# Keys of seven blocks by a seven-product scheme, with sums of x made by adding transfers

## The chip, the cores and the metric

The kernel runs on one core of one Trainium2 chip. The metric is device time in microseconds; a kernel's time is the median of its runs. Engines are named as in the profile: PE (matmul), PEld (its weight loads), DVE (vector), ACT (scalar), POOL and SP (here only issuers of transfers).

## What is computed

Two non-local blocks follow one another on x of 4 x 128 x 96 x 96, float32. Each does the following for every image:

```python
g_x     = maxpool2(conv1x1(x, g_w, g_b))          # 64 x 2304, after pooling
theta_x = conv1x1(x, theta_w, theta_b)            # 64 x 9216
phi_x   = maxpool2(conv1x1(x, phi_w, phi_b))      # 64 x 2304
f    = einsum('bqc,bck->bqk', theta_x, phi_x)     # 9216 queries, 2304 keys
attn = softmax(f, axis=-1)
y    = einsum('bqk,bkc->bqc', attn, g_x)
out  = conv1x1(y, W_w, W_b) * inv + (bn_beta - bn_mean * inv) + x
```

Four images and two layers make eight blocks. What the text calls the keys of a block is phi_x and g_x together: a 128 x 128 weight (64 rows of g, 64 of phi) times 9216 pixels, and a 2 x 2 maximum.

## The kernel before

**Blocks, pairs, steps.** The eight blocks stand in the order (image, layer) 00, 10, 01, 20, 11, 30, 21, 31. A block has 9 pairs; a pair is two tiles of 512 queries. The program is one loop over t, 648 steps; a pair takes 9 steps (NB), each with two tiles (KB) of 128 keys. Two pairs make a cycle of 18 steps (CYCLE); s is t modulo 18. Instruction order on PE, DVE, ACT and SP is that of the program; each engine takes its own in that order and waits by semaphores.

**A step.** `scores` of two key tiles (PE, L400), each followed by `exp` (ACT, L406); between the two stands `first`, a slot for other PE work, and after them `second`. Then `add_up` of the two exp tiles (DVE, L415), with a slot `take` between them that evacuates what PE made in the slots. Then `values` (PE, L423) of the two key tiles of the step before. Behind these come the tail pieces: `turn` (transposes and reduces of the exp sums, s = 8, 9 and 4, 5), `add_halves` (12 and 2), `invert` (13 and 6), `normalise` (1 and 10), each for the even and the odd pair, and transposes of keys.

**Quarters of the array.** Every matmul is 64 rows by 64 columns, so four run side by side. `scores` and `values` issue one for each quarter. A float32 matmul of the program is two records in the profile.

**The slots.** `thetas` of two pairs at s = 5 and 6; the W matmuls (`multiply`, L517) at s = 3 and 12, with ACT adding the shift (L528) and POOL adding the result to x in place by an adding transfer (L532); and keys.

**Keys before.** The keys of block n + 1 are made while block n runs. A chunk is 512 pixels, 128 keys; `chunks` does two of them with four matmuls in `first` and four in the next step's `second` (L236), into the two banks of the pool `ps_misc` that theta and W use as well. `take` reduces each bank by the 2 x 2 maximum into a tile `gphi` (DVE, L262). There are nine such calls a block, three in a cycle (`KEYS = (15, 17, 31)`), so keys take three of every four or five cycles. Every third call is followed by `centred` and `copied` (ACT, L336 and L342: phi less its mean, into both halves of the partitions of `phi`) and by `square` (DVE, L353: 32 x 32 transposes of g into `gT`). Block 0's keys are made at the start.

**Denominators.** `invert` sends the reciprocals by SP as two rows into the tile `turned` (L496) and from there, each row to 64 partitions, into half of `halves` (L501). `normalise` waits for that.

**Pools.** exp tiles have `EXPS = 7` buffers, `halves` two, `ps_sc` two double banks.

Of the kernel before, what the change touches and what calls it, by code (L numbers as in the profile page):

```python
# [16 lines left out]
P = 128  # L17
# [7 lines left out]
GT = 6  # L25
# [9 lines left out]
KB = 2  # L35
NB = NKT // KB
FIRST = 6
KEYS = (15, 17, 31)
THETAS = 5


TURNS, HALVES, INVERT = (8, 4), (12, 2), (13, 6)
NORM, PROJECT = (1, 10), (3, 12)
SQ = 32
EXPS = 7
WARM = (5, 3)
CYCLE = 2 * NB
ORDER = ((0, 0), (1, 0), (0, 1), (2, 0), (1, 1), (3, 0), (2, 1), (3, 1))
# [5 lines left out]
def shifted_blocks(ctx: ExitStack, tc: tile.TileContext, x: bass.AP, layers, out: bass.AP, flag):  # L54
# [47 lines left out]

    notes = const.tile([P, len(ORDER) * NP + 1, 2], F32, name="notes")
    nc.vector.memset(notes, 0.0)
    limits = const.tile([P, 2], F32, name="limits")
    for i, limit in enumerate((SUM_MAX, 1.0 / SUM_MIN)):
        nc.vector.memset(limits[:, i : i + 1], limit)
# [29 lines left out]
    class Layer:  # L137
# [3 lines left out]
            self.l, self.p, self.col = l, p, {}  # L141

        def load_gphi(self, engines):
            self.gphi_nat = prep.tile([2 * CI, C], F32, name=f"gphi_nat_{self.l}")
            for i, key in enumerate(("g", "phi")):
                engines[i].dma_start(out=self.gphi_nat[ts(i, CI), :], in_=self.p[f"{key}_w"])

        def load_theta(self, engine):
            self.theta_nat = prep.tile([CI, C], F32, name=f"theta_nat_{self.l}")
            engine.dma_start(out=self.theta_nat, in_=self.p["theta_w"])  # L150

        def load_W(self, engine):
            self.W_nat = prep.tile([C, CI], F32, name=f"W_nat_{self.l}")
            engine.dma_start(out=self.W_nat, in_=self.p["W_w"])
            self.g_b = prep.tile([C, CI], F32, name=f"g_b_{self.l}")
            engine.dma_start(out=self.g_b, in_=self.p["g_b"].partition_broadcast(C))

        def make_std(self):
# [15 lines left out]
        def steps_gphi(self):  # L174
            self.gphi = const.tile([C, 2 * CI], F32, name=f"gphiT_{self.l}")
            return turned(self.gphi, self.gphi_nat)

        def steps_theta(self):
            self.theta = const.tile([C, CI], F32, name=f"thetaT_{self.l}")
            return turned(self.theta, self.theta_nat)  # L180

        def steps_W(self):

            self.W = const.tile([2 * CI, C], F32, name=f"WT_{self.l}")
            self.W_bn = prep.tile([C, CI], F32, name=f"W_bn_{self.l}")
            self.inv = prep.tile([C, 1], F32, name=f"inv_{self.l}")
            twice = lambda: nc.scalar.copy(self.W[CI:, :], self.W[:CI, :])
            return [self.make_scale] + turned(self.W[:CI, :], self.W_bn) + [twice, self.make_shift]
# [51 lines left out]
    class Block:  # L240


        def __init__(self, xt, w, store, name):
            self.xt, self.w, self.store, self.name = xt, w, store, name

        def begin_keys(self):
            name = self.name
            self.gphi = kvp.tile([P, NK], F32, tag="gphi", name=f"gphi_{name}", bufs=1)
            self.phi = kvp.tile([P, NK], F32, tag="phi", name=f"phi_{name}")
            self.gT = kvp.tile([P, NKT, CI], F32, tag="gT", name=f"gT_{name}")  # L250
            self.centre = kvp.tile([P, 1], F32, tag="centre", name=f"centre_{name}")

        def chunk(self, k, rows):

# [93 lines left out]
        def square(self, i, k):  # L348
# [3 lines left out]
            for c in range(CI // 32):  # L352
                nc.vector.transpose(  # L353
                    self.gT[ts(k, 32), tiles, ts(c, 32)], g[ts(c, 32), tiles, ts(k, 32)]
                )

    class Pair:


# [33 lines left out]
            self.th = work.tile([P, QT], F32, tag="theta", name=f"theta_{self.name}", bufs=3)  # L393
            nc.scalar.activation(self.th, ps, AF.Identity, bias=self.blk.w.col["theta_b"])

        def scores(self, k):
            ps = ps_sc.tile([P, PT], F32, tag="sc", name=f"sc_{self.name}_{k}")
            for c in range(2):
                for h in range(2):
                    nc.tensor.matmul(  # L400
                        ps[ts(c, CI), ts(h, QT)],
                        lhsT=self.blk.phi[ts(h, CI), ts(2 * k + c, CI)],
                        rhs=self.th[ts(h, CI), :], start=True, stop=True,
                    )
            e = work.tile([P, PT], F32, tag="exp", name=f"exp_{self.name}_{k}", bufs=EXPS)
            nc.scalar.activation(e, ps, AF.Exp, bias=nshift)  # L406
            self.es[k] = e
# [56 lines left out]
        def turn(self, h):  # L464

            if h == 0:
                self.turned = work.tile(
                    [P, QT], F32, tag="turned", name=f"turned_{self.name}"
                )
                self.parts = work.tile(  # L470
                    [P, SQ], F32, tag="parts", name=f"parts_{self.name}", bufs=1
                )
            nc.vector.transpose(self.turned, self.sum[:, ts(h, QT)])  # L473
            nc.vector.tensor_reduce(  # L474
                self.parts[:, ts(h, QT // SQ)],
                self.turned.rearrange("p (b k) -> p b k", k=SQ), AX.X, ALU.add,
            )

        def invert(self):

            four = work.tile(
                [SQ, P // SQ, SQ], F32, tag="four", name=f"four_{self.name}", bufs=1
            )
            both = work.tile([SQ, 2, SQ], F32, tag="both", name=f"both_{self.name}", bufs=1)
            for k in range(P // SQ):
                nc.vector.transpose(four[:, k, :], self.parts[ts(k, SQ), :])  # L486
            nc.vector.tensor_reduce(
                both[:, 0, :], four.rearrange("p k q -> p q k"), AX.X, ALU.add
            )
            nc.vector.reciprocal(both[:, 1, :], both[:, 0, :])  # L490
            nc.vector.tensor_reduce(notes[:SQ, self.number, :], both, AX.X, ALU.add)
            self.rc = self.halves[:, QT:]
            n = QT // SQ
            for h in range(2):
                row = self.turned[h * CI : h * CI + 1, :]
                nc.sync.dma_start(  # L496
                    out=row.rearrange("o (b k) -> o b k", k=SQ), in_=both[ts(h, n), 1, :]
                )
            for h in range(2):
                row = self.turned[h * CI : h * CI + 1, :]  # L500
                nc.sync.dma_start(  # L501
                    out=self.rc[ts(h, CI), :],
                    in_=row.unsqueeze(1).to_broadcast([1, CI, QT]),
                )

        def add_halves(self):
# [99 lines left out]
        [(w, key) for w in ws for key in rest] + [(ws[1], "theta_b")], "other", nc.sync  # L606
    )
    ws[0].load_W(nc.sync)
    ws[1].load_gphi((nc.sync, nc.sync))
    ws[1].load_theta(nc.sync)  # L610
    ws[1].load_W(nc.sync)

    blocks = []
    for b, l in ORDER:
# [14 lines left out]
    def busy(n):  # L629
        for i in range(n):  # L630
            nc.tensor.matmul(warm[:, :P], lhsT=ident, rhs=ident, start=True, stop=True)  # L631


    begin(0)
    b0 = blocks[0]
    busy(WARM[0])
    ws[0].make_gphi()
    busy(WARM[1])
# [22 lines left out]
    xs[1] = load_x(1)  # L661


    after = {8: [other_cols]}
    for i, step in enumerate(ws[0].steps_W()):
        after[10 + i] = [step]
    steps = ws[1].steps_gphi() + ws[1].steps_theta() + ws[1].steps_W()
    for i, step in enumerate(steps):
        after[CYCLE + i // 3 * CYCLE + (2, 7, 11)[i % 3]] = [step]

    keys = {2 * j: (0, FIRST + j) for j in range(NB - FIRST)}
    squares = {k: [(1, k)] for k in range(4)} | {5: [(2, k) for k in range(4)]}
    spreads, centres = {}, {}
    for n in range(1, len(blocks)):
        cycle = (n - 1) * NP * NB // CYCLE * CYCLE
        for j in range(NB):
            t = cycle + KEYS[j % len(KEYS)] + j // len(KEYS) * CYCLE
            keys[t] = (n, j)
            if j == 0:
                centres[t + 2] = blocks[n]  # L680
            if j % len(KEYS) == len(KEYS) - 1:
                spreads[t + 2] = (blocks[n], j // len(KEYS))
    loads = {4 * NB + 7: 2, 31 * NB + 6: 3}
    late = len(pairs) - 2

# [5 lines left out]
    for t in range(total + 1):  # L691
        q, s = 2 * (t // CYCLE), t % CYCLE
        even, odd = pairs[q : q + 2] if t < total else (None, None)
        first, second, take = None, *pending
        pending = (None, None)
        if t in keys:
            n, i = keys[t]
            if n and i == 0:
                begin(n)
            first, *pending = blocks[n].chunks(i)  # L700
        elif t < total and s == (THETAS if q else THETAS + 1):
            if q < late:
                first, *pending = thetas(pairs[q + 1 : q + 3])
            else:
# [11 lines left out]
                xs[loads[t]] = load_x(loads[t])  # L716
        for i in range(KB):
            if t < total:
                pairs[now].scores(j * KB + i)
            if i == 0 and first:  # L720
                first()
        if second:
            second()
        for i in range(KB):
            if t < total:
                pairs[now].add_up(j * KB + i)
            if i == 0 and take:
                take()
        if t == 0:
            b0.batch(FIRST - 1)  # L730
# [21 lines left out]
                even.normalise()  # L752
        if t == total - 1:
            odd.last_denominators()
        if t in centres:
            centres[t].centring(KB)
        for i, k in squares.get(t, []):
            b0.square(i, k)
        for k in range(KT // 32):
            if t - k in spreads:  # L760
                blk, i = spreads[t - k]
                if k == 0:
                    blk.centred(ts(i, GT * KT))
                if k == 1:
                    blk.copied(ts(i, GT * KT))
                blk.square(i, k)
        for step in after.pop(t, []):
            step()
    assert not after

    good = const.tile([P, 2], F32, name="good")

# [319 lines left out]
```

## Time and profile before

| | |
|---|---|
| median of 3 runs | 2492.54 us (2492.3 to 2493.02) |
| profiled execution | 2492.8 us, span 2490.9 us |
| granted PE clock | 0.999 |
| PE busy | 2482.2 us |
| DVE busy | 2054.9 us (82%) |
| ACT busy | 1623.3 us (65%) |
| keys on PE (L236) in the chain | 5% of the span |
| DMA | 97.23 MB, mean 39 GB/s |

The span runs from the first to the last instruction. Busy shares are means over the whole span; what a stage allows is read from stretches of it. A cycle with keys and one without differ, so the two kinds are read apart. Some records are missing from the trace.

### The profile page before, as it was taken

The numbers are of one execution on the slowest core, as the hardware profiler recorded it, in microseconds if no ns is written. First come the engines' busy times: TensorE is split into PE (matmuls) and PEld (weight loads), VectorE is DVE, ScalarE is ACT, GpSimd is POOL, SyncE is SP. The second block draws the span as 40 slices with busy tenths as digits, with TensorE's granted clock in tenths as the row PEclk, the third lists the DMA queues.
The fourth block names the chain that finished last, engine by engine and source line by source line (L and its number), as shares of the span: only waits on it lengthen the run. The fifth ranks groups of instructions, "written<-read, shape, count | busy, mean of one in ns | idle before, by whom it ended". The sixth has DMA issues, their size and how long they took to land.

```text
span 2490.9 us, 53893 instructions
## 1 busy us (share of the span) xinstructions
PE 2482.2 (100%) x23055; PEld 1111.8 (45%) x23055; DVE 2054.9 (82%) x2587; ACT 1623.3 (65%) x1653; POOL 79.7 (3%) x110
## 2 busy tenths in 40 slices
PE   9999999999999999999999999999999999999998
PEld 5444444444444444444444444444444444444444
DVE  7888888888788888888878888788887888877788
ACT  6666666666666666666766666666666666666665
POOL 0000000000000000000000000000000000000000
PEclk9999999999999999999999999999999999999999
DMA  4124222222222322233222223222222232233323
GB/s 158 16 25 102 19 27 27 24 25 19 27 35 39 44 35 36 35 37 88 26 22 31 42 41 44 30 32 27 26 24 26 27 44 40 43 44 43 35 36 61
DMA packets 37219, 97.23 MB, mean 39 GB/s; under 512 B 9698, under 2 KB 10604, under 8 KB 36972
## 3 DMA queue, kind: packets, MB, share of 16 engines
q1 hardware_dynamic: 21828, 39.11, 18.5%
q0 software_dynamic: 14976, 54.53, 9.5%
q8 instruction: 182, 2.98, 0.5%
q14 instruction: 65, 0.53, 0.1%
q10 hardware_dynamic: 168, 0.07, 0.0%
HBM read 19.21 MB, written 18.87 MB: 15 GB/s over the span
## 4 chain that ended last, share of the span: by engine, by line
PE 100%; DVE 0%; ACT 0%; POOL 0%; issue 0%; DVEq 0%; POOLq 0%
PE av L423 45%; PE sc L400 45%; PE gphi_ps L236 5%; PE W_ps L517 2%; PE theta_ps L236 2%; PE gphi_ps L278 0%; PE warm_ps L631 0%; PE den_last_ps L440 0%; DVE x L574 0%; PE W_ps L559 0%; ACT exp L406 0%; PE theta_ps L380 0%; PE theta_ps L368 0%; DVE halves L552 0%; PE warm_ps L122 0%
## 5 line engine op out<-in xcount | busy, mean ns | idle before, releaser
L406 ACT ACTIVATE exp<-sc,nshift 128x1024 f32<-128x1024 f32 x1296 | 1385.1, 1112 | 787.4 <-PE sc L400 785.9
L415 DVE TENSOR_TENSOR sum<-sum,exp 128x1024 f32<-128x1024 f32 x1151 | 1408.5, 1224 | 336.8 <-ACT exp L406 283.5
L400 PE MATMUL sc<-theta,phi 64*64 64x512 f32 x10368 | 1520.9, 589 | 0.4 <-ACT exp L406 0.4
L423 PE MATMUL av<-exp,gT 64*64 64x512 f32 x10368 | 1465.3, 589 | 0.0
L400 PEld LDWEIGHTS sc<-theta,phi 64*64 64x64 f32 x10368 | 563.5, 133 | 614.8 <-issue 604.7
L423 PEld LDWEIGHTS av<-exp,gT 64*64 64x64 f32 x10368 | 545.7, 133 | 616.0 <-issue 590.7
L236 PE MATMUL gphi_ps<-x,gphiT 64*64 64x512 f32 x1056 | 185.4, 589 | 0.0
L532 POOL DMA_DIRECT2D x<-halves x70 | 59.9, 856 | 2240.6 <-ACT halves L528 2207.2
L413 DVE TENSOR_TENSOR sum<-exp,exp 128x1024 f32<-128x1024 f32 x72 | 88.2, 1225 | 35.7 <-ACT exp L406 35.0
L262 DVE TENSOR_REDUCE gphi<-gphi_ps 128x128 f32<-128x512 f32 x144 | 92.5, 681 | 27.7 <-PE gphi_ps L236 24.8
L430 ACT COPY halves<-av 128x1024 f32<-128x1024 f32 x71 | 71.9, 1012 | 50.3 <-PE av L423 50.3
L474 DVE TENSOR_REDUCE parts<-turned 128x16 f32<-128x512 f32 x142 | 97.4, 686 | 4.9
L473 DVE STREAM_TRANSPOSE turned<-sum 128x512 f32<-128x512 f32 x142 | 100.3, 706 | 1.2
L517 PE MATMUL W_ps<-halves,WT 64*64 64x512 f32 x568 | 99.3, 589 | 0.0
L236 PE MATMUL theta_ps<-x,thetaT 64*64 64x512 f32 x560 | 98.6, 589 | 0.0
L236 PEld LDWEIGHTS gphi_ps<-x,gphiT 64*64 64x64 f32 x1056 | 61.1, 133 | 62.5 <-issue 50.5
L528 ACT ACTIVATE halves<-W_ps,shift 128x512 f32<-128x512 f32 x140 | 88.7, 693 | 0.0
L353 DVE STREAM_TRANSPOSE gT<-gphi 32x192 f32<-32x192 f32 x192 | 70.7, 368 | 3.5
L486 DVE STREAM_TRANSPOSE four<-parts 32x32 f32<-32x32 f32 x284 | 56.4, 198 | 2.9
L508 DVE TENSOR_TENSOR halves<-halves 128x512 f32<-128x512 f32 x71 | 48.7, 686 | 0.0
L511 DVE TENSOR_TENSOR halves<-halves 128x512 f32<-128x512 f32 x71 | 48.7, 686 | 0.0
L517 PEld LDWEIGHTS W_ps<-halves,WT 64*64 64x64 f32 x568 | 33.5, 133 | 33.5 <-issue 33.5
(77 smaller groups left out, 278.2 us busy)
## 6 DMA issues: line engine op xcount, KB each, us to landing
x<-halves POOLq DMA_DIRECT2D x70, 512.0 KB, 4.5
halves<-turned SPq DMA_DIRECT2D x142, 128.0 KB
out_dram<-x POOLq DMA_DIRECT2D x34, 512.0 KB, 2.9
x<-in_x_dram SPq DMA_DIRECT2D x18, 768.0 KB
x<-in_x_dram SPq DMA_DIRECT2D x12, 384.0 KB
turned<-both SPq DMA_DIRECT2D x142, 2.0 KB
out_dram<-x SPq DMA_DIRECT2D x1, 512.0 KB
out_dram<-x SPq DMA_DIRECT2D x2, 256.0 KB
```

Source lines behind the costliest of these rows:

```text
L236: nc.tensor.matmul(out, lhsT=lhsT, rhs=rhs, start=step == 0, stop=step == 1)
L262: nc.vector.tensor_reduce(self.gphi[:, ts(k, KT)].rearrange("p (h w) -> p h w", w=w), ps.rearrange("p (h a w b) -> p h w a b", a=2, b=2, w=w),
L400: nc.tensor.matmul(ps[ts(c, CI), ts(h, QT)], lhsT=self.blk.phi[ts(h, CI), ts(2 * k + c, CI)], rhs=self.th[ts(h, CI), :], start=True, stop= ...
L406: nc.scalar.activation(e, ps, AF.Exp, bias=nshift)
L413: nc.vector.tensor_add(self.sum, self.es[0], e)
L415: nc.vector.tensor_add(self.sum, self.sum, e)
L423: nc.tensor.matmul(self.av[ts(h, CI), ts(r, QT)], lhsT=self.blk.gT[ts(r, CI), k, :], rhs=e[ts(r, CI), ts(h, QT)], start=(k == 0), stop=(k ...
L430: nc.scalar.copy(self.halves, self.av)
L473: nc.vector.transpose(self.turned, self.sum[:, ts(h, QT)])
L474: nc.vector.tensor_reduce(self.parts[:, ts(h, QT // SQ)], self.turned.rearrange("p (b k) -> p b k", k=SQ), AX.X, ALU.add,)
L517: nc.tensor.matmul(self.pss[h][ts(c, CI), :], lhsT=self.blk.w.W[ts(h, CI), ts(c, CI)], rhs=self.y[ts(h, CI), :], start=True, stop=True,)
L528: nc.scalar.activation(self.halves[:, ts(h, QT)], self.pss[h], AF.Identity, bias=self.blk.w.shift,)
```

## The change

The keys of blocks 2 to 8 are made in units of 16 image rows instead of chunks; a unit's 1536 pixels are four parts of 384 (upper and lower eight rows by `c`, and within them the halves by `i`). Weight and pixels are taken as 2 x 2 matrices of 64-row blocks, and a Strassen scheme makes the four products' sums from seven products instead of eight. For this

- `steps_mixed` prepares sums and differences of the weight's blocks, once for each layer;
- `build` and `build_rest` make the sums of x's blocks in two tiles `sums`, by four plain transfers from SP and four adding transfers from POOL for each unit; a part of one sum is copied to the lower partitions (`half`);
- a unit has four stages on PE, in the slots of the steps `UNITS`: `first`, `third` and `fourth` are four matmuls of 384 columns each; `second` and `second_rest` are two of 192 columns each, which use only the upper or only the lower rows of the array. In that step the scores of the second key tile are issued row by row (`rowwise`);
- DVE adds the products up in a tile `stage` (`first_sum` to `fourth_sum`) and then takes the maximum from there (`pool`), 768 columns at once; ACT copies one bank (`first`);
- `spread` (ACT) and `square` (DVE) write the keys in a new layout, with half of phi's keys in each of two planes; `keys_of` reads it. Block 0 keeps the old one (`whole`).

To go with it, `turned` has one buffer, the reciprocals pass through rows of `stage` in four pieces (eight transfers instead of four), `EXPS` is 6, the odd pair's W matmuls stand at s = 13, the first cycle's theta at 6, and the loads and preparations of the second layer's weights come later. The core of the diff:

```diff
-KEYS = (15, 17, 31)
-THETAS = 5
+UR = 16
+NU = H // UR
+UN = 4 * W
+UK = UN // 4
+UB = 2 * UK // 32
+TB = NKT // 2
+UNITS = ((15, 16, 18, 20), (25, 26, 28, 30))
+BUILD = 9
+AFTER = ((1, 1, 2, 4, 5), (1, 2, 2, 3, 4))
+THETAS = (6, 5)
-NORM, PROJECT = (1, 10), (3, 12)
+NORM, PROJECT = (1, 10), (3, 13)
-EXPS = 7
+EXPS = 6
+    stage = const.tile([P, NK], F32, name="stage")
+    sums = [const.tile([P, 2, UN], F32, name=f"sums_{i}") for i in range(2)]
...
+        def pixels(self, i, rows):
+            some = self.blk.xt[rows, ts(self.u, UR * W)]
+            return some.rearrange("p (c i n) -> p c i n", c=2, i=2)[:, :, i, :]
+        def build(self):
+            low, high = slice(0, CI), slice(CI, P)
+            one, two = sums
+            nc.sync.dma_start(out=one, in_=self.pixels(0, slice(0, P)))
+            nc.sync.dma_start(out=two[high], in_=self.pixels(1, low))
+            for dst, src in (
+                (one[high], self.pixels(0, low)), (two[high], one[high]),
+                (one[low], self.pixels(1, low)),
+            ):
+                nc.gpsimd.dma_start(out=dst, in_=src, accum_op=ALU.add)
+            nc.sync.dma_start(out=self.half, in_=two[high, :, UN // 2 :])
+        def build_rest(self):
+            nc.sync.dma_start(out=two[low], in_=self.pixels(1, high))
+            nc.gpsimd.dma_start(out=two[low], in_=two[high], accum_op=ALU.add)
+        def both(self, *some):
+            for c in range(2):
+                for bank, lhsT, rhs in some:
+                    nc.tensor.matmul(
+                        bank[ts(c, CI), :UN], lhsT=lhsT, rhs=rhs[:, c, :], start=True, stop=True
+                    )
+        def part(self, lhsT, rhs, i):
+            for c in range(2):
+                nc.tensor.matmul(
+                    self.pss[i][ts(c, CI), ts(i, UN // 2)], lhsT=lhsT, rhs=rhs[:, c, :],
+                    start=True, stop=True,
+                )
+        def first(self):
+            self.pss = two_banks(f"unit_ps_{self.name}")
...
+            self.both(
+                (self.pss[0], w[low, :CI], self.pixels(1, low)),
+                (self.pss[1], w[high, :CI], self.pixels(1, high)),
+            )
+            nc.scalar.copy(self.s[:, 0, :], self.A)
+        def first_sum(self):
+            nc.vector.tensor_add(self.s[:, 1, :], self.s[:, 0, :], self.B)
+        def second(self):
+            self.part(self.blk.w.mixed[CI:, 0, :], sums[1][CI:, :, : UN // 2], 0)
+        def second_rest(self):
+            self.part(self.blk.w.mixed[:CI, 2, :], self.half, 1)
+        def second_sum(self):
+            for i in range(2):
+                dst, cols = self.s[:, 0, ts(i, UN // 2)], ts(i, UN // 2)
+                nc.vector.tensor_add(dst, dst, self.pss[i][:, cols])
...
+        def third_sum(self):
+            nc.vector.tensor_add(self.s[:, 3, :], self.s[:, 0, :], self.A)
+            nc.vector.tensor_sub(self.s[:, 2, :], self.B, self.s[:, 3, :])
+            nc.vector.tensor_sub(self.s[:, 0, :], self.B, self.s[:, 0, :])
...
+        def fourth_sum(self):
+            nc.vector.tensor_add(self.s[:, 3, :], self.s[:, 3, :], self.A)
+            nc.vector.tensor_add(self.s[:, 0, :], self.s[:, 0, :], self.B)
+        def pool(self, i):
+            nc.vector.tensor_reduce(
+                self.keys[:, ts(i, 2 * UK)].rearrange("p (h w) -> p h w", w=W // 2),
+                self.s[:, ts(i, 2), :].rearrange(
+                    "p i (h a w b) -> p (i h) w a b", a=2, b=2, w=W // 2
+                ),
+                AX.XY,
+                ALU.max,
+            )
+        def spread(self):
...
+            for m, n, k, t in self.parts():
+                dst = planes[:, :, t : t + n, ts(k, 32)]
+                nc.scalar.activation(
+                    dst[:, 0], src[:, m : m + n, :], AF.Identity, bias=self.blk.centre
+                )
+                for h in range(2):
+                    nc.scalar.copy(dst[ts(1 - h, CI), 1], dst[ts(h, CI), 0])
...
-        def scores(self, k):
+        def scores(self, k, rowwise=False):
+            for i in range(4):
+                h, c = divmod(i, 2) if rowwise else (i % 2, i // 2)
...
+            n = QT // SQ // 2
+            first = CI + self.number % 2 * SQ
+            for i in range(4):
+                row = stage[first + i : first + i + 1, NK - UN :][:, : QT // 2]
                 nc.sync.dma_start(
+                    out=row.rearrange("o (b k) -> o b k", k=SQ), in_=both[ts(i, n), 1, :]
                 )
...
+            at = [cycle + u // 2 * 2 * CYCLE // 2 + i for i in UNITS[u % 2]]
+            if u == 0:
+                later(cycle + BUILD, lambda n=n: begin(n))
+                later(cycle + BUILD, unit.build)
+                later(cycle + BUILD, unit.build_rest)
+            else:
+                later(free[0], unit.build)
+                later(free[1], unit.build_rest)
+            free = at[2:]
+            when = [at[3] + i for i in AFTER[u % 2]]
+            later(when[0], lambda unit=unit: unit.pool(1))
+            later(when[1], lambda unit=unit: unit.pool(0))
+            later(when[2], unit.spread)
+            for i in range(2):
+                later(when[3 + i], lambda unit=unit, i=i: unit.square(i))
...
-                pairs[now].scores(j * KB + i)
+                pairs[now].scores(j * KB + i, rowwise=stage_of == 1 and i == 1)
-            if i == 0 and take:
+            if i == (stage_of == 1) and take:
                 take()
```

`later` puts a piece of work behind the tail pieces of a step. In the steady cycle the stages of the even units stand at s = 15, 16, 0 and 2, those of the odd ones at 7, 8, 10 and 12; an odd unit is built behind the even one's third and fourth stage (s = 0 and 2), an even one behind the odd one's (s = 10 and 12), and a block's first at s = 9.

## The prediction

> **What bounds the kernel now.** I read the busy shares first, then the chain of waits, then the groups, then busy time by stretch, then single lines and tiles.
>
> ```profile
> PE 2482.2 (100%) x23055; PEld 1111.8 (45%) x23055; DVE 2054.9 (82%) x2587; ACT 1623.3 (65%) x1653; POOL 79.7 (3%) x110
> PE 100%; DVE 0%; ACT 0%; POOL 0%; issue 0%; DVEq 0%; POOLq 0%
> ```
>
> PE is idle for 2490.9 - 2482.2 = 8.7 us in all, and the chain never leaves it. So a matmul less is time less, as long as nobody makes PE wait. How long a matmul takes on this path is read from the chain in order of time and from the stretches:
>
> ```profile
> 60.48 1.72 PE av L423 x16
> 1053.05:1123.44 70.39, 70.39 (x664) 31.34 (x660) 58.67 (x74) 45.66 (x47) 1.71 (x2) 1.00 0.31 46
> 1191.25:1256.48 65.23, 65.23 (x615) 29.11 (x611) 53.78 (x65) 43.57 (x45) 1.71 (x2) 1.00 0.27 25
> ```
>
> The columns are stretch, us, then busy us (count) of PE, PEld, DVE, ACT, POOL. A matmul of the program is two records, and four matmuls, one for each 64x64 quarter of the array, are a group: 16 records in 1.72 us are two groups, 0.858 us each. One cycle (18 steps, two pairs) without keys is 76 groups (72 scores and values, 2 theta, 2 W): 76 x 0.858 = 65.2, as the second stretch has it. With six chunks of keys it is 82 groups = 70.4, as the first has it. PE therefore runs at its rate without a hole, with or without keys, and DVE has 70.39 - 58.67 = 11.7 us to spare in a key cycle.
>
> **What PE loses.** Before, blocks 2 to 8 do 18 chunks each, one group a chunk: 7 x 18 = 126 groups, 108.1 us. After, a unit (16 image rows; three chunks' worth) is twelve 384-column matmuls and four 192-column ones: (12 x 384 + 4 x 192) / 2048 = 2.625 groups instead of 3. For 42 units that is 15.75 groups x 0.858 = 13.5 us. This is the whole gain: 0.64 us in each of 21 key cycles.
>
> Does a shorter matmul cost its share? The row nearest is the 256-column one at the end:
>
> ```profile
> L559 PE MATMUL W_ps<-halves,WT x32: 376/376/427, 2481.9 to 2483.8; 64*64 64x256 f32 x32
> ```
>
> 32 starts lie in 1.9 us, 61 ns apart with a wait for input included; half of the 512-column spacing (1.72 us / 16 = 107.5 ns) is 54 ns. So a short record costs 0 to 7 ns extra. There are 32 records a unit: 0 to 9.4 us over 42 units. I take 0, as the starts that don't wait are nearest to the case; 9.4 goes to the range.
>
> The Trainium skill (TensorEngine Tiling (Array Packing), section Instruction Overhead) speaks against the change: it gives each matmul about 60 cycles of overhead on trn2, so that cutting work into smaller matmuls is not free. An estimate from it, at the 2.4 GHz that Trainium Kernel Development and Optimization gives in its section NeuronCore Architecture, is 25 ns for each of the 8 extra records of a unit, 8.4 us in all, and a time of about 2488; the L559 row shows at most 7 ns.
>
> **What DVE gains.** Rows: a 128x512 add 686 ns, a 128x256 add with a PSUM operand 416, so a 128x384 add 553 and a 128x192 one 350; a reduce 681 for 512 columns and slope as the add, so 950 for 768. A unit has six 384 adds, two 192 adds, two pools: 3.32 + 0.70 + 1.90 = 5.92 us. Two units a cycle 11.84, for six pools of 0.681 = 4.09 taken away. Transposes go from 8 x 0.368 = 2.94 to about 3.4 a cycle (two units of six are cut in two parts). So 58.67 - 4.09 - 2.94 + 11.84 + 3.4 = 66.9 us of DVE in a cycle of 82 - 0.75 = 81.25 groups = 69.7 us of PE: 96%. That is an upper end, since independent DVE operations overlap:
>
> ```profile
> 561.52 0.21 DVE L491 TENSOR_REDUCE notes<-both 32x2 f32<-32x64 f32 x1
> 561.66 1.20 DVE L415 TENSOR_TENSOR sum<-sum,exp 128x1024 f32<-128x1024 f32 x1
> 562.79 1.27 DVE L262 TENSOR_REDUCE gphi<-gphi_ps 128x128 f32<-128x512 f32 x2
> 565.54 2.56 DVE L415 TENSOR_TENSOR sum<-sum,exp 128x1024 f32<-128x1024 f32 x2 [0.35 <-ACT exp L406]
> ```
>
> The reduce at 562.79 starts 0.07 us before the add ends, while two adds on one sum take 2.56 us, 0.1 more than two alone. Twenty new operations at 0.07 less, and a chunk or unit sum between the two adds of a step, which saves that 0.1, bring it to about 65.5. DVE fits, with 3 to 4 us left in a cycle where it had 11.7.
>
> Step by step it fits less well. The heaviest steps are s=13 (two adds 2.45, invert 1.71, pool 0.95 = 5.1 us against 5 groups = 4.29 on PE) and s=6 (2.45 + 1.71 + 0.74 = 4.9 against 4.29). DVE falls about 0.8 us behind there and makes it up in s=11, s=17 and s=1. Who waits for a late DVE: PE, before second_rest (for first_sum, a step earlier), third and fourth (two steps earlier) and the W matmuls at s=3 and s=13 (for fourth_sum, one step); with a step of 3.4 to 4.3 us and sums of 0.55 to 1.66 us, 2 us of lateness are free at each. Tightest is ACT's copy in first at s=15, which overwrites what pool(0) at the end of s=14 still reads; ACT behind it holds exp, and 1.5 us later PE. I put 0.5 us in all on this.
>
> EXPS from 7 to 6 costs nothing: an exp tile lives until values one step later, so 4 of the 6 are in use and DVE may be a step behind.
>
> **What ACT gains.** Per unit one 128x384 copy (about 0.48 by the 1012 of 1024 columns) and a spread of 1.2 to 1.8 us: 3.7 us a cycle for 1.77 taken away. ACT goes from 45.7 to 47.6 of 69.7. Hidden.
>
> **What the queues gain.** Each unit issues four DMAs on SP and four on POOL. Their chain is load sums, add on POOL, add on POOL, copy of half on SP. Prices, from the groups and the tile view:
>
> ```profile
> x<-halves POOLq DMA_DIRECT2D x70, 512.0 KB, 4.5
> L532 POOL DMA_DIRECT2D x<-halves x70: 847/852/995, 104.5 to 2459.8; - x70
> L501 SPq DMA_DIRECT2D halves<-turned x142: 498/516/2141, 77.6 to 2458.7; - x142
> ```
>
> The new ones move 192 to 384 KB, so 4.5 us a link is an upper end: four links 18 us, plus issue about 2 = 20. The shortest window is from third at s=10 to second_rest at s=16: 24 us (31 for the other unit). Hidden, with 4 us left at the upper end. Queued behind on SP, which stands still for some 10 us until the second add has landed, are invert's DMAs, now eight at 0.5 to 0.6 instead of four. The builds at s=0, 9 and 10 end before invert at s=6 and s=13. The rows of reciprocals came 11 us after the first issue (DMA busy from 605 to 613 us for an issue at 602.3); now about 13.5, and normalise of the odd pair comes four steps, 15.3 us, later. POOL's x<-halves at s=3 and s=13 wait behind a build's adds for 2 to 6 us; their halves tile is wanted 5 steps later. The two mid-run loads of x share the rings for 20 us each, and the builds behind them still land a step early. All at nothing; without the cover, each us late is a us of PE, 21 or 42 times.
>
> POOL issues eight more DMAs a cycle, beside DVE's adds. The row for that, 1151 two-input adds beside 104 POOL transfers:
>
> ```profile
> L415 DVE TENSOR_TENSOR sum<-sum,exp x1151: 1201/1225/1228, 24.3 to 2474.2; 128x1024 f32<-128x1024 f32 x192
> ```
>
> At most 3 ns over the median, so the sum keeps nothing for it. The Trainium skill (SBUF — State Buffer, section Who interferes with whom) says otherwise for one case: a DVE operation with two SBUF inputs and a GpSimd instruction that reads SBUF lock each other out. If issuing an adding transfer were such a case, an estimate by it and by the issue's 0.85 us is 6.8 us of DVE a key cycle, 73.7 against 69.7 on PE, and 21 x 4 = 84 us more.
>
> **The sum.** Span 2490.9 - 13.5 + 0.5 = 2477.9; the profiled execution took 2492.8, 1.9 outside the span: 2479.8. The median of the runs, 2492.54, is 0.3 lower: **2479.5**. The measurement can tell about 0.2%, 5 us, from no change.
>
> **The rivals.**
> *The quarter pairs don't overlap.* second uses only the two upper-row quarters, second_rest only the lower two; the rowwise order of the scores between them is to let them run under each other. The trace has no such half-filled stretch. If each holds the array alone, they cost 2 x 0.32 instead of 0.32 us: 42 x 0.32 = 13.5 us, and the gain is gone: 2492.5. Against it: quarters start independently in all the groups. 8%.
> *Some loss on PE:* short records at 7 ns (9.4 us), or DVE lateness of 0.1 to 0.4 us a cycle: 2483 to 2488. 10%.
> *DVE becomes the bound (slower).* If a new sum costs as a 512-column one (0.686) and a pool as two (1.36), a unit is 1.6 us more, a cycle 66.9 + 3.2 = 70.1, and with the uneven steps PE waits about 1.5 to 2 us a cycle: 21 x 1.75 = 37 us on 2479, 2516. It decides from about 69 us of DVE in a key cycle. For it: 96%. Against it: slopes are known from four rows. 8%.
> *The adding chain is late (slower).* From 24 us on, which needs 5.5 us a link, PE stands at second: 1 us late in half the units is 21 us: 2500. For it: a stretch of up to 10.5 us to landing exists. Against it: a third to three quarters of the bytes. 6%.
>
> **How the numbers follow.** The forecast, 2478 to 2482.5, has 68%. With the loss case it is 78%, faster by over 0.2%; the unpaired case, 8%, is no change; the two slower ones 14%. The range reaches from 2478 (no DVE loss and 1 us for anything unseen) over the loss case to 2489.
>
> **What would show it.** Right: key cycles of 69.7 us, PE 100%, DVE 94 to 96% in them, no wait of PE for stage or sums. Wrong: steps s=8 and 16 longer than 3.75 us (pairing), PE waits named DVE stage, or DMA sums.

## The result, and the profile after

The changed kernel takes 2535.35 us (median of 6 runs, 2528.13 to 2541.08), the kernel before 2492.53. The ratio is 1.017, 95% interval 1.0151 to 1.0189: 43 us slower, where the forecast was 13 us faster. The profiled execution took 2539.5 us, span 2537.7.

The page's busy shares and its chain come first again:

```profile
PE 2487.6 (98%) x23391; PEld 945.2 (37%) x23391; DVE 2190.6 (86%) x2947; ACT 1671.8 (66%) x1836; POOL 233.9 (9%) x278
PE 73%; DMA 16%; DVE 6%; issue 2%; ACT 2%; SPq 2%; POOL 0%; DVEq 0%; POOLq 0%; ACTq 0%
```

PE was idle for 8.7 us before; now it is 2537.7 - 2487.6 = 50.1 us. That is 41 of the 60 us by which the profiled execution misses its forecast of 2479.8; the rest lies in time that counts as busy, up to 12 us of it at half clock (last section). So the busy time does not show the matmul time that was saved; the key cycles do. The chain, which never left PE before, now spends 16% of the span in transfers. Stretches of one cycle (columns as before: us, then busy us and count of PE, PEld, DVE, ACT, POOL, then the granted clock, the DMA share and GB/s):

```profile
1074.71:1144.46 69.75, 69.75 (x677) 26.27 (x672) 65.52 (x90) 47.39 (x52) 9.01 (x10) 1.00 0.55 68
592.04:657.28 65.24, 65.24 (x613) 23.25 (x608) 53.14 (x61) 43.59 (x44) 1.72 (x2) 1.00 0.32 25
```

A key cycle that nothing disturbs lasts 69.75 us, PE without a hole, DVE 65.5, ACT 47.4: the forecast's own figures. So most of the loss is not in the new work. It is in a few places where PE stands, which the waits name (engine, line, waited for: us in total, times, longest):

```profile
ACT halves L613 <- DMA x<-halves: 49.8, 17, 9.2
PE av L606 <- ACT halves L613: 29.3, 14, 7.5
PE unit_ps L441 <- DMA sums<-sums: 3.4, 1, 3.4
```

The first two are one chain. ACT copies av to a halves tile (L613) so that PE may start the next pair's values (L606); it waits for the transfer that adds an older halves tile to x (L716), because there are two such tiles. The third line, one wait, is the longest of PE's own for sums. One such place, by the timeline of POOL, SP and ACT in order of time (start us, us, engine, line, what, idle before and releaser); s=13 of cycle 9 begins at 704.5:

```profile
704.23 1.95 POOL L422 DMA_DIRECT2D sums<-x  x2 [31.11 <-DMA sums<-x]
707.75 0.82 POOL L422 DMA_DIRECT2D sums<-sums  x1 [1.57 <-DMA sums<-x]
711.80 0.60 SPq L423 DMA_DIRECT2D stage<-sums  x1
712.44 0.61 SPq L429 DMA_DIRECT2D sums<-x  x1
713.15 2.80 SPq L680 DMA_DIRECT2D stage<-both  x4
715.76 0.80 POOL L430 DMA_DIRECT2D sums<-sums  x1 [7.19 <-DMA stage<-both]
716.12 9.46 SPq L685 DMA_DIRECT2D halves<-stage  x4
716.46 1.03 POOL L716 DMA_DIRECT2D x<-halves  x1
730.67 1.01 ACT L613 COPY halves<-av 128x1024 f32<-128x1024 f32 x1 [3.47 <-DMA x<-halves]
```

ACT had W's result ready at 708.9. But SP stands at L423 until the second add has landed (711.80), the load for the third part of the build goes out behind it (L429), POOL's add waits for that load (L430, 715.76), and x<-halves stands behind the add: out at 716.46 instead of some 708.9. (The profile names stage<-both, the row writes that run beside the load. In 41 of the 42 builds the add starts 0.54 to 0.57 us after the load has landed, whatever name stands there.) At that moment invert's four broadcasts go out as well (L685; with 9.46 us for four issues, SP itself is held). x<-halves lands after 14.1 us. The tile view has the range over all 70 of them, first for the kernel before, then for the change:

```profile
DMA to landing us min/median/max: 4.5/4.5/10.5
```

```profile
DMA to landing us min/median/max: 4.5/5.3/14.7
```

In the 20 cycles with a build at this place, x<-halves of s=13 goes out 8.5 to 21.1 us after the step's start (median 10.7) and takes 14.1 us in the median; in the 15 others the medians are 4.7 and 4.5. The copy at s=1 could run 23.3 us after that start in a full key cycle; the landing is at 25.0 in the median.

**Where the 60 us are.** Summing the lengths of steps over what they last undisturbed gives, against the forecast's 2479.8 for the profiled execution:

| place | us |
|---|---|
| s=1 behind a late x<-halves, 14 cycles (25.3), and a slow s=2 after three of them (2.0) | 27.3 |
| around the two loads of x: cycle 2 s=16, 17 (7.7), cycle 3 s=1 (4.0), cycle 16 s=10, 11 (9.8) | 21.5 |
| the end (83.3 us after the start of the last cycle, 79.1 before) | 4.2 |
| cycle 0, s=10 and 11 | 2.2 |
| small waits in cycles 1 to 5 and a few later ones | 5.5 |

Together 60.7, of which the forecast had allowed 0.5.

### The profile page after: what moved, and what is told of

The parts are those of the page before. It is cut to its first block, busy times and chain, and to the rows that moved or that the text cites. A ratio compares the mean times of both kernels' runs of the same rounds, so it can differ in the third digit from the quotient of the medians.

```text
span 2537.7 us, 56492 instructions
## 1 busy us (share of the span) xinstructions
PE 2487.6 (98%) x23391; PEld 945.2 (37%) x23391; DVE 2190.6 (86%) x2947; ACT 1671.8 (66%) x1836; POOL 233.9 (9%) x278
## 4 chain that ended last, share of the span: by engine, by line
PE 73%; DMA 16%; DVE 6%; issue 2%; ACT 2%; SPq 2%; POOL 0%; DVEq 0%; POOLq 0%; ACTq 0%
PE av L606 33%; PE sc L584 33%; DMA x<-halves 8%; DMA sums<-x 4%; DVE sum L598 3%; PE unit_ps L435 2%; PE theta_ps L268 2%; PE W_ps L701 2%; DMA sums<-sums 1%; ACT exp L589 1%; DMA halves<-stage 1%; SPq L680 1%; SPq L685 1%; ACT halves L613 1%; DMA stage<-both 0%
## 5 line engine op out<-in xcount | busy, mean ns | idle before, releaser
L584 PE MATMUL sc<-theta,phi 64*64 64x512 f32 x10368 | 1291.8, 590 | 3.1 <-ACT exp L589 3.0
L606 PE MATMUL av<-exp,gT 64*64 64x512 f32 x10368 | 1249.8, 592 | 29.4 <-ACT halves L613 29.3
L606 PEld LDWEIGHTS av<-exp,gT 64*64 64x64 f32 x10368 | 418.1, 133 | 715.1 <-issue 651.6
L584 PEld LDWEIGHTS sc<-theta,phi 64*64 64x64 f32 x10368 | 424.2, 133 | 680.0 <-issue 589.5
L422 POOL DMA_DIRECT2D sums<-x x84 | 82.4, 1160 | 836.9 <-DMA sums<-x 535.2
L716 POOL DMA_DIRECT2D x<-halves x70 | 70.8, 1011 | 836.9 <-ACT halves L712 836.8
L613 ACT COPY halves<-av 128x1024 f32<-128x1024 f32 x71 | 71.9, 1012 | 75.1 <-DMA x<-halves 49.8
L495 DVE TENSOR_REDUCE stage<-stage 128x192 f32<-128x768 f32 x84 | 77.8, 940 | 0.0
L536 DVE STREAM_TRANSPOSE gT<-stage 32x192 f32<-32x192 f32 (+1 forms) x224 | 71.5, 319 | 3.8
L268 PE MATMUL theta_ps<-x,thetaT 64*64 64x512 f32 x560 | 74.0, 589 | 0.0
L435 PE MATMUL unit_ps<-sums,mixed 64*64 64x384 f32 x504 | 70.2, 484 | 0.0
L430 POOL DMA_DIRECT2D sums<-sums x42 | 33.8, 805 | 303.9 <-DMA stage<-both 131.4
```

What stands on the lines that cost most here:

```text
L268: nc.tensor.matmul(out, lhsT=lhsT, rhs=rhs, start=step == 0, stop=step == 1)
L435: nc.tensor.matmul(bank[ts(c, CI), :UN], lhsT=lhsT, rhs=rhs[:, c, :], start=True, stop=True)
L584: nc.tensor.matmul(ps[ts(c, CI), ts(h, QT)], lhsT=self.blk.keys_of(k, c, h), rhs=self.th[ts(h, CI), :], start=True, stop=True,)
L606: nc.tensor.matmul(self.av[ts(h, CI), ts(r, QT)], lhsT=self.blk.gT[ts(r, CI), k, :], rhs=e[ts(r, CI), ts(h, QT)], start=(k == 0), stop=(k ...
L613: nc.scalar.copy(self.halves, self.av)
```

## The experiments

The theory: x<-halves stands in POOL's queue behind a build's last add, goes out late, and then shares the DMA engines with invert's broadcasts; PE waits for the halves tile. Rivals: A, W at s=13 collides with the broadcasts by itself; B, the adding chain or DVE is late; C, POOL's order alone; D, the four-piece rows. The time before stands at 2492.6 to 2492.8 in these runs.

**The add behind x<-halves.**

```diff
-                later(free[1], unit.build_rest)
+                later(free[1] + 1, unit.build_rest)
```

> The second half of a build (its load on SP and its adding transfer on POOL) one step later, so that at s=13 x<-halves stands ahead of that add in POOL's queue. Theory (x<-halves waits behind that add, goes out 4 to 9 us late and then shares the DMA engines with invert's broadcasts, 12 to 15 us instead of 4.5): x<-halves of s=13 goes out 4.7 us after the step's start and lands in about 5, the waits at s=1 and s=2 in the cycles after key stages (27 us) go, those around the loads of x and the end stay: about 2508 us. Rival A (moving W to s=13 is enough to collide with the broadcasts): no change, 2535. Rival B (the adding chain itself, or DVE, is late for PE): no change or a few us.

2523.37 us, ratio 1.0121 (1.0104 to 1.0138): 12 us better than the change, not 27. Where the edit acts, the theory holds to the letter:

```profile
711.07 0.80 POOL L430 DMA_DIRECT2D sums<-sums  x1 [7.18 <-DMA stage<-both]
711.76 1.04 POOL L716 DMA_DIRECT2D x<-halves  x1
```

```profile
ACT halves L613 <- DMA x<-halves: 19.5, 6, 4.0
PE unit_ps L435 <- DMA sums<-sums: 6.9, 6, 4.2
```

Of 17 waits of ACT for x<-halves six are left (the second fence, waits). They follow cycles 4, 9, 13, 18, 22 and 27, where a block's first build is issued whole at s=9, which the edit does not move; the first fence, POOL's timeline, shows one of them. In the other key cycles x<-halves goes out at 4.7 us and takes about 5, but for the one after the first load of x. The miss is the last line: fourth at s=2 now waits for the delayed sum. The steps s=2 are 13.7 us too long in all (6.1 of it after the second load of x); the profile names 6.9 us as this wait. The expectation had left out both.

**A third halves tile.**

```diff
-EXPS = 6
+EXPS = 5
...
-                self.halves = work.tile([P, PT], F32, tag="halves", name=f"halves_{self.name}")
+                self.halves = work.tile(
+                    [P, PT], F32, tag="halves", name=f"halves_{self.name}", bufs=3
+                )
...
```

> Three halves tiles instead of two; to make room, five exp tiles instead of six. Transfers and their order stay. Theory: x<-halves is as late as before and lands in 12 to 15 us, but nobody waits for it: the waits at s=1 (29 us with the one after a load of x) and the one of 9.5 us at s=10 after the second load of x go, the 6.7 us for sums after the first load and 4 us at the end stay: about 2495. Rival B (adding chain or DVE late): little change, 2530 or more; more still if five exp tiles are too few for a DVE that falls behind.

2505.36 us, ratio 1.005 (1.0033 to 1.0067): 30 us better than the change, 10 less than expected. x<-halves goes out and lands as late as ever (14.2 us in the median), and not one wait of ACT for it is left; no step at s=1 or 2 is long. Of the 26 us over the forecast, 10.5 are still around the loads of x, and the end costs 7, not 4. Five exp tiles cost nothing that shows. Rival B is out as the cause of the waits at s=1: transfers, products and sums are all there.

**Without the broadcasts of the even pair.**

```diff
-            for i in range(4):
+            for i in range(4 if self.number % 2 else 0):
                 ...
-            nc.vector.tensor_mul(self.y, self.y, self.rc)
+            if self.number % 2:
+                nc.vector.tensor_mul(self.y, self.y, self.rc)
+            else:
+                nc.vector.tensor_sub(self.y, self.y, self.y)
```

> The four broadcasts of invert are left out for the even pair of each cycle, and normalise of that pair subtracts y from itself instead of multiplying it by the reciprocals: an operation of the same size. This part of the computation is changed. The row writes, POOL's order and W at s=13 stay. Theory (late issue and collision together): x<-halves of s=13 still goes out 8 to 13 us after the step's start but lands in about 5 us; the waits at s=1 go (27 us), 4 us at the end too: about 2504. Rival C (POOL's order alone makes x<-halves late, the broadcasts do not matter): the waits at s=1 stay, only the 4 us at the end go, 2531.

2493.79 us, ratio 1.0005 (0.9995 to 1.0015): a larger gain than expected, since the waits for x<-halves after the loads of x go too. The issue is as late as in the change (10.9 us after the step's start in the median); the transfer takes 5.2 us instead of 14.1:

```profile
705.71 0.80 POOL L430 DMA_DIRECT2D sums<-sums  x1 [7.25 <-DMA stage<-both]
706.40 1.03 POOL L719 DMA_DIRECT2D x<-halves  x1
```

```profile
DMA to landing us min/median/max: 4.5/5.2/11.7
```

Rival C falls: late issue without the broadcasts costs PE nothing. With the kernel of the first experiment, both halves of the theory are needed and each is shown by itself. The Trainium skill says in DMA: Bandwidth & Descriptors, section Issuing engines are not separate DMA queues, that transfers started by different engines run on the same 16 DMA engines and interleave. The trace agrees: from first to last packet the broadcasts alone take 9.6 us in cycles without builds, x<-halves alone lands in 4.5, and the 14.1 of x<-halves beside them is as long as the two together.

**W at s=13 in the kernel before.** The first try changed PROJECT alone:

> The kernel before with one number changed: W of the odd pair at s=13 instead of s=12, as the change has it. Theory: without adds on POOL x<-halves goes out 4.7 us after the step's start and has landed before the broadcasts begin at about 10: no change, 2492 to 2494. Rival A (W beside the broadcasts of the same step is enough): waits at s=1 in all 35 cycles, 1 to 4 us each, 2520 or more.

It took 2474.01 us, ratio 0.9926 (0.9909 to 0.9943), but tells nothing of the rival: a chunk of keys holds s=13 in 21 cycles, where the loop then passes W over, so W of 21 odd pairs is left out. (21 x 0.858 us = 18.0; the time fell by 18.6.) The second moved that chunk:

```diff
-KEYS = (15, 17, 31)
+KEYS = (15, 17, 29)
-NORM, PROJECT = (1, 10), (3, 12)
+NORM, PROJECT = (1, 10), (3, 13)
```

> The kernel before with W of the odd pair at s=13 instead of s=12, and the chunk of keys that stood at s=13 and 14 at s=11 and 12. Theory: no adds stand on POOL, x<-halves goes out 4.7 us after the step's start and lands in 4.5 before the broadcasts begin at about 9: 2492 to 2495 (1 or 2 us at the end). Rival A (W beside the same step's broadcasts is enough): 1 to 4 us in each cycle, 2520 or more.

2492.68 us, ratio 1.0 (0.9991 to 1.0009). Rival A falls.

**The loads of x elsewhere.**

```diff
-    loads = {4 * NB + 7: 2, 31 * NB + 6: 3}
+    loads = {8 * CYCLE + 7: 2, 17 * CYCLE + 7: 3}
```

> The two mid-run loads of x moved to s=7 of the cycles 8 and 17, which have no key stages. Theory: a build's loads queue behind six 768 KB transfers, its adds and then x<-halves on POOL behind them; with the loads elsewhere the waits around them go (cycle 2: 7.7 us at s=16 and 17, cycle 3: 4.0 at s=1, cycle 16: 9.8 at s=10 and 11), the other waits at s=1 stay: 2535 - 21 = 2514. Rival B (the adding chain is late by itself): the wait for sums stays where it is.

2516.5 us, ratio 1.009 (1.0074 to 1.0105). All three places around the loads are gone but for 0.8 us at s=16. How they came about, by the changed kernel's timeline at the first load:

```profile
206.18 0.68 SPq L416 DMA_DIRECT2D sums<-x  x1
221.81 1.94 POOL L422 DMA_DIRECT2D sums<-x  x2 [38.92 <-DMA sums<-x]
233.37 0.81 POOL L430 DMA_DIRECT2D sums<-sums  x1 [7.23 <-DMA stage<-both]
233.90 1.20 POOL L716 DMA_DIRECT2D x<-halves  x1
```

The build's load, issued behind six loads of 768 KB, lands some 15 us after its issue, so the adds, half and x<-halves all slip; second waits at s=16, values at s=1.

**Rows in two pieces.** stage is 128 columns longer, EXPS 5, and invert makes two rows of 512 and two broadcasts, as before:

```diff
-            for i in range(4):
-                row = stage[first + i : first + i + 1, NK - UN :][:, : QT // 2]
+            for i in range(2):
+                row = stage[first + i : first + i + 1, NK - UN :]
...
```

> Rows of reciprocals in stage again as two of 512 columns, so two broadcasts of 64 x 2 KB instead of four of 64 x 1 KB; stage is 128 columns longer and there are five exp tiles instead of six. Theory: the broadcasts take about 8 us alone (9.6 with four), x<-halves still goes out late and still meets them, but lands some 2 us sooner: in about 12 cycles 2 us less, and 2 to 4 us at the end: 2507 to 2520. Rival D (the four pieces are what makes x<-halves slow): it lands in 6 to 8 us and the waits at s=1 go: about 2502. Rival A or B: no change but at the end, 2532.

2518.06 us, ratio 1.0109 (1.0094 to 1.0125). The broadcasts alone take 9.6 us with two rows as with four, not 8. The 7.8 of before were with rows on partitions 0 and 64, and now both lie side by side above 64; that this makes the difference, no run tests by itself. So x<-halves does not get quicker (14.8 us in the median); by the medians it goes out 1.2 us sooner and lands 0.9 sooner. Rival D, a transfer slowed by the four pieces, falls for s=1. The margin is thin, though, and even so little earlier a landing takes PE's wait for values from 29.3 to 16.1 us:

```profile
PE av L606 <- ACT halves L613: 16.1, 12, 4.0
```

But the last cycle takes 78.9 us, as before the change: normalise there waits for the rows, and SP has four issues for them instead of eight (in the key cycle shown above 2.80 and 9.46 us of issuing; here 1.23 and 1.18).

**All of it.** Three halves tiles, five exp tiles, loads moved, and for the last cycle normalise of the odd pair at s=11 and W at s=12:

> Three halves tiles, five exp tiles, both loads of x in cycles without key stages, and in the last cycle normalise of the odd pair at s=11 and its W at s=12. Theory: of the 25 us of three halves tiles above 2480 the 11 at the loads go and 4 to 6 at the end: 2488 to 2491, below the kernel before.

2492.27 us, ratio 0.9995 (0.9986 to 1.0004), above the expected 2488 to 2491. The loads and s=1 are clean (7.3 us left in cycles 1 to 34), but the end stays at 83.8: W at s=12 now waits for the normalise at s=11. The rows were the cause there, not W's place. So, with W at s=13 again and without the edits of the last cycle:

```diff
+    whole = const.tile([P, NK + P], F32, name="stage")
+    stage, ident = whole[:, :NK], whole[:, NK:]
...
+            for i in range(2):
+                row = whole[first + i : first + i + 1, NK - UN :]
...
-            return [crossed, combined]
+            return [crossed, combined, copied]
```

> Three halves tiles and five exp tiles, both loads of x in cycles without key stages, rows of reciprocals as two of 512 columns (their last 128 columns lie in a tile that is idle by then), and the last copy of steps_mixed two steps after the first ones. W stays at s=13 in the last cycle too. Theory: at the end 79 us again instead of 84 (two_rows), 2 us less at s=10 of the first cycle, some 7 us of small waits in cycles 1 to 5 stay: 2484 to 2488, faster than the kernel before by 0.2 to 0.3%. If the broadcasts or the tile count were not the cause of what was left: 2491 or more.

2486.43 us, ratio 0.9975 (0.9966 to 0.9984): the change's gain, as far as it could be had.

```profile
PE 2472.3 (100%) x23391; PEld 1090.4 (44%) x23391; DVE 2192.9 (88%) x2947; ACT 1670.5 (67%) x1836; POOL 233.8 (9%) x278
PE 90%; DVE 7%; issue 1%; DMA 1%; ACT 1%; DVEq 0%; ACTq 0%; SPq 0%
```

```profile
DMA to landing us min/median/max: 4.5/5.3/15.5
```

The transfers are as slow as in the change (second fence, tile view of halves); DMA has left the chain because nobody waits for them. Of the 7 us above 2479.5, 6.5 are small waits in cycles 1 to 34, most of them in 1 to 5.

**One part alone, both ways.** Transfers without the products (the kernel before, with its own two rows and broadcasts, the builds' DMAs at the change's steps, and nobody reading sums), and products without the transfers:

> The kernel before, its keys still by eight products a chunk, with only the transfers of the builds added at the change's steps (nobody reads the sums), W of the odd pair at s=13, the third chunk at s=11 and 12, five exp tiles. Theory: x<-halves at s=13 again lands in 12 to 15 us in the cycles with builds; but here the steps from s=13 to s=1 are some 3 us longer, so the waits at s=1 are 0 to 2 us each (5 to 12 us in all); around the two loads of x 5 to 10 us each, since x<-halves stands behind adds that wait for their loads; a few at the end: 2508 to 2522. Rival B (the products, sums or DVE make the loss): 2493.

> The changed kernel without its builds: sums and half are set to zero once, so no adding transfers and no loads of sums (the keys lack those terms). Products, sums on DVE and all else stay. Theory: PE's 13.5 us come out; left are 2 us at s=10 of the first cycle, some 5 us in cycles 1 to 5 and 4 at the end: 2487 to 2491. Rival B (DVE or the products): 2500 or more.

Transfers alone: 2501.94 us, ratio 1.0036 (1.0022 to 1.0049), less than expected. Eight of the 9 us are one place, after the first load of x:

```profile
ACT halves L467 <- DMA x<-halves: 8.3, 1, 8.3
PE av L460 <- ACT halves L467: 6.4, 1, 6.4
```

Elsewhere x<-halves goes out 5.5 to 9 us after the step's start and takes 5 to 13.5, while the copy at s=1 comes at 25.1. I had taken the issue from the change; without PE reading sums, L429 waits for nobody and the add goes out sooner. Products alone: 2492.24 us, ratio 1.0 (0.999 to 1.0009), just above the expected 2487 to 2491. x<-halves goes out at 4.7 us and takes 4.5 in the median of the key cycles, with W at s=13 and the change's own four-piece rows, so rival A falls for these too. What lies over 2479.5 is the end (5.4), small waits (6.6) and cycle 0. The tile view of halves (the longest is in the last cycle):

```profile
DMA to landing us min/median/max: 4.5/4.5/12.4
```

So neither part makes the change's 56 us by itself.

## Why the prediction was wrong, point by point

**Right: PE.** 13.5 us of matmul time are gone, 0.64 us in each key cycle (70.39 before). A key cycle was to be 69.7 us and is 69.75; 81.25 groups at 0.858 make 69.71, so a short record costs no more than 0.04 / 64 us. The 8.4 us that the forecast worked out from the Trainium skill's 60 cycles a matmul (TensorEngine Tiling (Array Packing), section Instruction Overhead) are not to be seen; the measured cycle decides, and the L559 row was the better guide. Quarter pairs overlap: s=8 lasts 3.76 us.

**Right: DVE, ACT, and POOL beside DVE.** 65.5 and 47.4 us in a key cycle, as forecast (65.5, 47.6). The adds beside 278 POOL transfers keep their length, so no lock shows:

```profile
L598 DVE TENSOR_TENSOR sum<-sum,exp x1151: 1201/1225/1228, 24.8 to 2521.6; 128x1024 f32<-128x1024 f32 x192
```

**Wrong: "All at nothing" for the queues.** The step that failed is "POOL's x<-halves at s=3 and s=13 wait behind a build's adds for 2 to 6 us; their halves tile is wanted 5 steps later." The wait was a median 6 us (10.7 instead of 4.7), near the upper end. What was not asked is what x<-halves would meet 6 us later. Its price stayed at 4.5 us; beside the broadcasts it is 14.1. Wanted at 23.3, it lands at 25.0. The forecast had both facts in hand, invert's DMAs on SP at s=13 and W moved to s=13, but weighed each queue by itself. It had the stretch of 10.5 us to landing too, and used it for the wrong transfer.

**Wrong: "the builds behind them still land a step early".** Behind the loads of x, second waited for its sums and values for their halves tile: 21.5 us.

**Mis-sized: "I put 0.5 us in all".** Some 5.5 us of small waits, and 2.2 in cycle 0, where ACT stood in steps_mixed for a DVE result (its last copy two steps later: cycle 0 shorter by 0.9 us). The small waits are all still there in products alone (6.6 us), so the builds' transfers do not make them; their cause was not taken apart further.

**Not foreseen: the end,** 4.2 us from eight small transfers on SP in place of four.

**The rivals.** "The adding chain is late" had the right kind of cause, transfers, but its place was second waiting for sums; that happened after a load of x only. By the page of the changed kernel an adding transfer of a build lands after 4.0 to 4.7 us in the median, close to the forecast's upper end of 4.5 a link. The tile that ran out is one that the change does not touch.

## What to carry to other kernels

A transfer that is moved or queued behind others has a new time at which it goes out: look up what else is in flight then, on every queue, and price it beside that (here at the sum of both), not at the median of the one. Follow each delayed transfer to the buffer that it frees, and give its lateness and that buffer's next use in the same clock. Where the trace shows the new work running at the forecast's rate, look for the loss in old work that shares a queue with it; another buffer may then be cheaper than a better order.

## What the runs showed that was not expected

A short pause of PE can cost more than itself. In the changed kernel, after 2.28 us of waiting, the stretches by time read:

```profile
727.56:731.70 4.14, 1.90 (x20) 0.46 (x12) 0.90 (x1) 1.03 (x2) 0.00 (x0) 1.00 0.64 148
731.70:734.76 3.06, 3.02 (x16) 1.00 (x20) 1.92 (x2) 2.01 (x2) 1.23 (x2) 0.59 0.04 10
```

The granted clock (third from the right) is 0.59 of full speed in the mean of the second stretch, and 16 records that last 1.72 us take 3.06. The records of the clock have six stretches at half speed in that execution, 3.4 to 6.8 us each, 14.6 us lost in all; in the best kernel above (2486.43 us) one, at the very end, 2.2. So up to 12 of the 60 us are not waiting but its echo. Over the runs of this study, before the last cycle and between the modelled ends of matmuls, no pause of 2.0 us or less brought such a stretch; of the 21 from 2.03 to 4.2 us, 15 did.

The Trainium skill (TensorE: Matmul & The Clock Gate, section What's actually happening) gives one idle window of about 3.4 us as what throttles the clock. Here 2.05 us was enough at one place and 3.5 us was not at another; the length of a throttled stretch, 3.41 us or twice that, is the page's window. For this kernel the measured pauses decide.

Broadcasts of the same 256 KB took 7.8 us from rows on partitions 0 and 64 and 9.6 from rows on neighbouring partitions, in two pieces or four. With four pieces, one issue could hold SP for up to 7.4 us (2.1 before, 2.9 with two pieces on neighbouring partitions), so what stood behind it on SP slipped too.
